# A four-layer graph network on one core: the rows of layer 4 as plain float32 instead of two float32r halves

## The chip, the core and the metric

The kernel runs on one core of one Trainium2 chip. The metric is the device time of one execution in microseconds (us). Three runs of the kernel before gave 2556.82, 2551.59 and 2554.43 us, median 2554.43 us. The profiled execution took 2551.33 us, and its span, from the first to the last instruction in the profile, is 2549.5 us.

## The reference: what is computed

The input has 6250 nodes with 256 features each and 100,000 edges sorted by destination. After a layer norm and a relu come four graph layers without a nonlinearity between them, and a last matrix; the input is added back at the end:

```
def _sage_mean(h, src, dst, n, deg, W_self, W_neigh, b):
    msum = jax.ops.segment_sum(h[src], dst, num_segments=n)
    h_neigh = msum / jnp.clip(deg, 1.0)[:, None]
    return h @ W_self + h_neigh @ W_neigh + b
...
    h = _sage_mean(features, edge_src, edge_dst, n, deg, W1_self, W1_neigh, b1)
    h = _sage_pool(h, edge_src, edge_dst, n, deg, W2_pool, b2_pool, W2_self, W2_neigh, b2)
    h = _sage_gcn(h, edge_src, edge_dst, n, deg, W3_neigh, b3)
    h = _sage_mean(h, edge_src, edge_dst, n, deg, W4_self, W4_neigh, b4)
    return h @ W_fc + b_fc
h = jnp.maximum(_layernorm(x, axis=-1), 0.0)
x = x + _L0_gnn_ref(h, src, dst, ...)
```

Layer 4 is what the change is about. The kernel has multiplied the weights of layers 3 and 4 and of the last matrix together early on, so that layer 3 ends with 512 columns for a node: 256 that belong to the node itself (`xq`), and 256 whose mean over the node's incoming edges is still to be taken (`tab_s`). Layer 4 is then: output = x + xq + (sum of `tab_s` rows over the edges) / degree.

## The kernel before, in words

Nodes are cut into 49 tiles of 128 (d or s counts tiles). Destinations are very uneven: the first tiles have most of the edges. Each summing layer therefore has two ways of summing over edges, and both are products on TensorE (PE):

- **dense**, for the 23 destination tiles d below H4 = 23 (`dense`, line 589): for each pair (d, s) a 128 x 128 block of edge counts, built once and kept in HBM as fp8 (`tab_a`), is multiplied with the 128 rows of source tile s. That is 23 x 49 = 1127 products in layer 4. `stream` (line 1818) loads the count blocks on the ACT queue in chunks of 5 or 6 (tile `ac`) and ScalarE (ACT) widens them to 4 bytes (`af`, line 1838).
- **gather**, for the other 26 destination tiles (`sums`, line 503): the remaining edges come in 254 steps of 128. Each step fetches 128 rows with an indirect DMA on the GpSimd (POOL) queue into a ring of 14 places (line 525), VectorE (DVE) builds a 128 x 128 one-hot matrix of the destinations (`hot`, line 521), and PE multiplies the two (line 543 in layer 4). Four steps make one group in PSUM (`pg`), and for each destination tile that has edges in the group DVE adds the masked group to an accumulator `acc` (lines 575 and 577).

`sums` also sets the order: PE's program has one gather product, then so many dense products (4 or 5) that they end 8 steps before the gather ends. The dense products of the first four destination tiles with the first 23 source tiles, 92 in number, are put ahead of the first gather product (line 1976, `hub.advance(4 * H3)`).

A float32r product rounds its operands. So layer 3 splits each 256-column row v, in `halves` (line 322), into hi = float32r(v), a copy on ACT (line 325), and lo = v - hi, a subtraction on DVE (line 326), and stores 512 columns in `tab_s` (line 1913) beside `xq` (line 1914), both from SP's queue. In layer 4 (the branch `wide`) one float32r product of 512 columns yields both sums side by side, and DVE adds them: twice per destination and group at line 577, and twice per tile at line 1957, which is the end of the layer (`finish4`, then the store to `out`).

Where the rows of layer 4 lie for the dense products: tiles 0 to 22 and 33 to 42 stay in SBUF from layer 3 (`Z4`); tiles 23 to 32 and 43 to 48 are read back from `tab_s` in three loads (`resident`, line 1855) after layer 3.

For comparison with other float32 work: the weight products (`product`, line 271; the matmul is line 285, four products with 128 rows each are summed for a result) and the bias rows (`bias_rows`, line 298) run early in the program on plain float32 operands, some with 256 and some with 512 columns. Transposes by a matmul with the identity (line 1607 and others) are plain float32 too.

## Time and profile before

| what | value |
|---|---|
| median of three runs | 2554.43 us |
| profiled execution | 2551.33 us |
| its span | 2549.5 us |
| PE busy / DVE / POOL / ACT, share of the span | 85% / 80% / 68% / 51% |
| mean granted PE clock | 0.936 of full |
| gathers of layer 3, first to last start | 1845.5 to 2181.1 us |
| gathers of layer 4, first to last start | 2194.6 to 2530.0 us |

How to read the rows below. A row of the timeline is: start, duration, engine, line, operation, tile written<-tiles read, shape, count of instructions merged in it, and in brackets how long the engine had been idle and what ended that. A row by groups is: line, engine, operation, tiles, shape, count, then total busy us and mean ns of one, then idle time before them and what ended it. PE is a product, PEld the load of the stationary matrix into the array, which runs beside products. Products are pipelined: one record lasts longer than the distance to the next record's start, so the pace of PE is read from starts. A row by stretches gives for each engine the busy us and the count, then the granted PE clock, the mean busy share of the DMA engines and GB/s. SPq and ACTq are DMA issues.

### The profile page before, as it was taken

The page shows a single profiled execution, that of the slowest core. Times are in us where ns is not written, and L with a number is a line of the kernel's source. Part 1 is how long each engine was busy: PE and PEld are TensorE (multiplying, and loading weights), DVE is VectorE, ACT ScalarE, POOL GpSimd, SP SyncE. Part 2 cuts the span into 40 slices and gives each one's busy share as a digit, 9 for nine tenths or more (in the row PEclk, how much of TensorE's full clock was granted, in tenths as well). Part 3 has the DMA queues.
Part 4 walks back from the last instruction along what each step waited for, and adds up shares of the span by engine and source line. Part 5 has one row for each costly group of instructions (what it writes and reads, how often), then busy time and mean ns, then how long its engine had stood idle before and what let it go on. Part 6 is the DMA issues. An engine that isn't in the chain of part 4 may idle for free.

```text
span 2549.5 us, 35257 instructions
## 1 busy us (share of the span) xinstructions
PE 2171.2 (85%) x9379; PEld 1259.7 (49%) x9379; DVE 2044.3 (80%) x5490; ACT 1289.6 (51%) x2685; POOL 1732.9 (68%) x2018
## 2 busy tenths in 40 slices
PE   4789999999687565679999999896399999799987
PEld 2346666767443222234444444342144444488766
DVE  7899998876599899888989999788657778377656
ACT  5679988566378887765323333231112222354443
POOL 5466776667476776777667666677477777477775
PEclk9899999999898787899999999898699999899999
DMA  9667777678799999999999999999799999899996
GB/s 313 177 191 212 215 214 216 203 218 240 248 382 321 332 362 346 335 365 357 342 319 338 343 330 304 302 358 317 255 376 401 402 406 392 292 341 342 324 308 212
DMA packets 380302, 781.10 MB, mean 306 GB/s; under 512 B 56718, under 2 KB 176118, under 8 KB 380060
## 3 DMA queue, kind: packets, MB, share of 16 engines
q0 software_dynamic: 134800, 470.32, 55.4%
q1 hardware_dynamic: 155816, 216.23, 23.5%
q10 hardware_dynamic: 89476, 92.21, 10.9%
q8 instruction: 76, 1.25, 0.2%
q14 instruction: 134, 1.10, 0.1%
HBM read 569.93 MB, written 209.41 MB: 306 GB/s over the span
## 4 chain that ended last, share of the span: by engine, by line
PE 49%; DMA 26%; DVE 13%; issue 4%; ACT 4%; POOL 3%; ACTq 0%; SPq 0%; DVEq 0%; POOLq 0%
PE pd L606 8%; PE pd L601 8%; DMA X<-rows,srcIf 8%; PE pd L599 6%; DMA ring<-tab_r,srcE 6%; PE pm_prf L1620 4%; PE pm_hp L1203 3%; DVE run L1709 3%; PE pm_w L285 2%; PE pm_hp L1197 2%; DMA rows<-X 2%; PE pm_prf L1614 2%; PE pg L545 2%; PE pg L548 2%; PE pm_prf L1617 2%
## 5 line engine op out<-in xcount | busy, mean ns | idle before, releaser
L1728 POOL DMA_INDIRECT X<-rows,srcIf x782 | 743.2, 950 | 315.9 <-issue 143.2
L1709 DVE SCALAR_TENSOR_TENSOR run<-run,samef,X 128x512 f32<-128x512 f32 x758 | 572.9, 756 | 37.3 <-DMA X<-rows,srcIf 32.5
L525 POOL DMA_INDIRECT ring<-tab_h,srcT x402 | 390.8, 972 | 175.4 <-issue 49.6
L1838 ACT CAST af<-ac 128x640 fp32r<-128x640 fp8e4 (+2 forms) x299 | 216.3, 735 | 370.9 <-PE pd L606 143.8
L577 DVE SCALAR_TENSOR_TENSOR acc<-pg,M,acc 128x256 f32<-128x256 f32 (+2 forms) x556 | 282.8, 533 | 52.5 <-PE pg L548 41.7
L525 POOL DMA_INDIRECT ring<-tab_r,srcE x254 | 257.3, 1013 | 94.5 <-issue 33.0
L525 POOL DMA_INDIRECT ring<-tab_s,srcE x254 | 243.9, 960 | 105.1 <-PE pg L543 37.8
L1709 DVE SCALAR_TENSOR_TENSOR X<-X,samef,run 128x512 f32<-128x512 f32 x379 | 281.8, 744 | 34.0 <-issue 12.1
L548 PE MATMUL pg<-ring,hot 128*128 128x256 f32 (+1 forms) x656 | 292.3, 455 | 0.0
L606 PE MATMUL pd<-kept_rows,aw 128*128 128x512 f32 x529 | 271.0, 588 | 0.1
L1664 ACT CAST aw<-ae 128x512 fp32r<-128x512 fp8e4 x184 | 113.8, 620 | 255.8 <-PE pd L606 236.0
L545 PE MATMUL pg<-ring,hot 128*128 128x259 f16 (+1 forms) x656 | 209.4, 322 | 38.8 <-DMA ring<-tab_r,srcE 17.6
L601 PE MATMUL pd<-kept_rows,ae 128*128 128x512 f16 x529 | 209.2, 395 | 9.5 <-DMA ae<-tab_a 6.9
L521 DVE TENSOR_SCALAR hot<-iota_bf,keyE 128x128 fp32r<-128x128 bf16 x508 | 137.7, 298 | 79.6 <-PE pg L543 40.2
L1620 PE MATMUL pm_prf<-unf,hTf 128*128 128x512 f32 x384 | 191.3, 622 | 5.4 <-ACT hTf L1610 4.7
L606 PE MATMUL pd<-Z1h,af 128*128 128x256 f32 x588 | 195.5, 366 | 0.1
L599 PE MATMUL pd<-zt,af 128*128 128x512 f32 x598 | 165.0, 396 | 6.7 <-ACT af L1838 6.7
L548 PEld LDWEIGHTS pg<-ring,hot 128*128 128x128 f32 x656 | 129.0, 197 | 84.0 <-issue 68.5
L601 PEld LDWEIGHTS <-ae 128*128 128x128 fp8e4 x736 | 71.5, 97 | 191.8 <-issue 177.9
L601 PE MATMUL pd<-Z1l,A 128*128 128x259 f16 x588 | 159.8, 282 | 0.2 <-ACT A L379 0.2
L374 PE MATMUL pb<-hm,hs 128*128 128x392 bf16 x461 | 146.7, 344 | 13.2 <-DVE hm L368 11.4
L599 PE MATMUL pd<-z,af 128*128 128x512 f32 x529 | 145.8, 404 | 13.1 <-ACT af L1838 13.1
(415 smaller groups left out, 5028.2 us busy)
## 6 DMA issues: line engine op xcount, KB each, us to landing
rows<-X SPq DMA_DIRECT2D x385, 256.0 KB
rows<-hpf SPq DMA_DIRECT2D x49, 256.0 KB
th<-tab_t ACTq DMA_DIRECT2D x49, 256.0 KB
X<-rows,srcIf POOLq DMA_INDIRECT x782
ae<-tab_a SPq DMA_DIRECT2D x184, 64.0 KB
tab_a<-A ACTq DMA_DIRECT2D x15, 784.0 KB
ac<-tab_a ACTq DMA_DIRECT2D x138, 80.0 KB
tab_t<-th SPq DMA_DIRECT2D x37, 256.0 KB
```

The costliest lines, as they stand in the source:

```text
L374: nc.tensor.matmul(hold[0], hots[0], hots[1], start=(k == 0), stop=(k == k_of[w] - 1))
L525: nc.gpsimd.indirect_dma_start(out=ring[:, j % deep, :].bitcast(F32), out_offset=None, in_=table, in_offset=bass.IndirectOffsetOnAxis(ap=s ...
L545: nc.tensor.matmul(pg[:, : F + counts], hot[j].bitcast(BF16)[:, 1::2], X.bitcast(F16)[:, 2 * F : 3 * F + counts], start=(k == 0), stop=False)
L548: mm = nc.tensor.matmul(pg[:, :F], hot[j], X[:, :F], start=False, stop=(k == n - 1))
L577: nc.vector.scalar_tensor_tensor(acc[d], half, m, acc[d], op0=ALU.mult, op1=ALU.add)
L599: nc.tensor.matmul(hold[0], a[0], z, start=(s == ss[0]), stop=(s == ss[-1]))
L601: nc.tensor.matmul(hold[0][:, : F + extra], a[1], z[1][:, : F + extra], start=(s == ss[0]), stop=False)
L606: nc.tensor.matmul(hold[0][:, :F], a[0], z[0], start=False, stop=(s == ss[-1]))
L1620: nc.tensor.matmul(pm, hT[:, c, :], un[:, c, :], start=False, stop=(c == KH - 1))
L1709: nc.vector.scalar_tensor_tensor(put, held, st, row, op0=ALU.mult, op1=ALU.max)
L1728: nc.gpsimd.indirect_dma_start(out=X[:, k, :], out_offset=None, in_=tab_p, in_offset=bass.IndirectOffsetOnAxis(ap=srcI[:, t : t + 1], axis=0),
L1838: nc.scalar.copy(wide[i][:, :n, :], got[i][:, :n, :])
```

## The change

Layer 3 stores its 256 columns as they are: `halves` is gone, `tab_s` has 256 columns, the store reads the accumulator itself, and ACT copies the columns once more for those tiles that stay in SBUF. In layer 4 the ring, the one-hot matrices, the widened count blocks and the kept rows are plain float32, and each product has 256 columns (the new branch `plain` in `sums` and `dense`). DVE adds one result where it added two. Of the rows, tiles 0 to 22 and 29 to 48 stay in SBUF; only 23 to 28 are read back, in one load.

```
-    tab_s = dram.tile([NP, 2 * FO], F32, name="tab_s")
+    tab_s = dram.tile([NP, FO], F32, name="tab_s")
...
-        ring = pool.tile([P, deep, table.shape[1]], F32R, name="ring", bufs=1)
+        form = F32 if plain else F32R
+        ring = pool.tile([P, deep, table.shape[1]], form, name="ring", bufs=1)
...
-            hot[j] = pool.tile([P, P], F32R, name="hot", bufs=ahead + spare_hots)
+            hot[j] = pool.tile([P, P], form, name="hot", bufs=ahead + spare_hots)
...
                 if wide:
                     nc.tensor.matmul(pg, hot[j], X, start=(k == 0), stop=(k == n - 1))
+                elif plain:
+                    mm = nc.tensor.matmul(pg, hot[j], X[:, : F + counts], start=(k == 0),
+                                          stop=(k == n - 1))
...
             if wide:
                 nc.tensor.matmul(hold[0], a[0], z, start=(s == ss[0]), stop=(s == ss[-1]))
+            elif plain:
...
+                nc.tensor.matmul(hold[0], a[0], z[:, : F + extra],
+                                 start=(s == ss[0] and s != own), stop=(s == ss[-1]))
...
-        z4_kept = ((33, 38), (38, 43))
-        z4_late = ((H3, 28), (28, 33), (43, NT))
+        z4_kept = ((29, 34), (34, 39), (39, 44), (44, NT))
+        z4_late = ((H3, 29),)
...
-                q2 = Z4[d] if d in Z4 else wk.tile([P, 2 * FO], F32R, name="q2")
-                halves(q[:, FO:], FO, q2)
-                nc.sync.dma_start(tab_s[d * P : (d + 1) * P, :], q2.bitcast(F32))
+                if d in Z4:
+                    nc.scalar.copy(Z4[d], q[:, FO:])
+                nc.sync.dma_start(tab_s[d * P : (d + 1) * P, :], q[:, FO:])
                 nc.sync.dma_start(xq[d * P : (d + 1) * P, :], q[:, :FO])
...
-                for c in range(0, acc.shape[1], FO):
-                    nc.vector.scalar_tensor_tensor(xr[:n, :], acc[:n, c : c + FO],
-                                                   rmean[:n, d : d + 1], xr[:n, :],
-                                                   op0=ALU.mult, op1=ALU.add)
+                nc.vector.scalar_tensor_tensor(xr[:n, :], acc[:n, :], rmean[:n, d : d + 1],
+                                               xr[:n, :], op0=ALU.mult, op1=ALU.add)
...
-            order = [*z4_first, *z4_kept, *z4_late]
+            order = [*z4_first, *z4_kept[:2], *z4_late, *z4_kept[2:]]
...
-                                    lambda acc, d=d: todo.append(done4(d, acc)), wide=True))
+                                    lambda acc, d=d: todo.append(done4(d, acc)), plain=True))
```

PE's program at the start of layer 4, before: the last two of the 92 products with kept rows, the first five gather products, then dense and gather products in turn (`z` are kept rows, `zt` rows of a group of tiles, `af` count blocks, `pd` the dense sums).

```order
L599 MATMUL pd<-z_21_22793,af 128x512
L599 MATMUL pd<-z_22_22913,af 128x512
L543 MATMUL pg<-ring,hot 128x512 x5
L599 MATMUL pd<-zt_19884,af 128x512 x5
L543 MATMUL pg<-ring,hot 128x512
L599 MATMUL pd<-zt_19884,af 128x512 x4
```

The same place in the changed program.

```order
L601 MATMUL pd<-z_21_22734,af 128x256
L601 MATMUL pd<-z_22_22851,af 128x256
L540 MATMUL pg<-ring,hot 128x256 x5
L601 MATMUL pd<-zt_19884,af 128x256 x5
L540 MATMUL pg<-ring,hot 128x256
L601 MATMUL pd<-zt_19884,af 128x256 x4
```

Nothing moved: the products stand in the same places and in the same number, each with 256 columns in place of 512.

SP's program at the end of layer 3, before: the stores of the last two tiles, then the three loads of the rows that are read back.

```order
L1914 DMA xq<-acc 128x256
L1913 DMA tab_s<-q_22976 128x512
L1914 DMA xq<-acc 128x256
L1913 DMA tab_s<-q_23001 128x512
L1857 DMA zt_23200<-tab_s 128x5x512
L1857 DMA zt_23202<-tab_s 128x5x512
L1857 DMA zt_23204<-tab_s 128x6x512
```

The same place in the changed program.

```order
L1917 DMA tab_s<-acc 128x256
L1918 DMA xq<-acc 128x256
L1917 DMA tab_s<-acc 128x256
L1918 DMA xq<-acc 128x256
L1861 DMA zt_23131<-tab_s 128x6x256
```

The store of `tab_s` now stands ahead of that of `xq`, both read the accumulator, and one load of six tiles with 256 columns is left of three with 16 tiles and 512 columns.

More of the change, by code (lines that the diff above doesn't have):

```diff
@@ L320, in load_col @@
         return t
-    def halves(v, F, put):
-        hi, lo = put[:, :F], put[:, F:]
-        nc.scalar.copy(hi, v)
-        nc.vector.tensor_sub(lo, v, hi.bitcast(F32))
     def merged(*lists):
@@ L525, in gather @@
             nc.gpsimd.indirect_dma_start(
-                out=ring[:, j % deep, :].bitcast(F32),
+                out=ring[:, j % deep, :] if plain else ring[:, j % deep, :].bitcast(F32),
                 out_offset=None, in_=table,
@@ L587, in sums, with dense @@
         del todo[:]
-    def dense(ss, block, rows, F, psd, done, extra=0, wide=False, own=None):
+    def dense(ss, block, rows, F, psd, done, extra=0, wide=False, plain=False, own=None):
         hold = {}
@@ L599, in run @@
                 nc.tensor.matmul(hold[0], a[0], z, start=(s == ss[0]), stop=(s == ss[-1]))
+            elif plain:
+                if s == own:
+                    nc.tensor.matmul(hold[0], ident, z, start=(s == ss[0]), stop=False)
+                nc.tensor.matmul(hold[0], a[0], z[:, : F + extra],
+                                 start=(s == ss[0] and s != own), stop=(s == ss[-1]))
             else:
@@ L1816, in fast_path, with stream @@
     upto2.close()
-    def stream(pool, chunks, wide_pool, deep=4, ahead=2):
+    def stream(pool, chunks, wide_pool, deep=4, ahead=2, form=F32R):
         got = {}
@@ L1854, in resident @@
     def resident(pool, table, F, s0, s1):
-        zt = pool.tile([P, s1 - s0, table.shape[1]], F32R, name=f"zt{s0}", bufs=1)
-        nc.sync.dma_start(zt.bitcast(F32),
+        plain = table.shape[1] == F
+        zt = pool.tile([P, s1 - s0, table.shape[1]], F32 if plain else F32R, name=f"zt{s0}", bufs=1)
+        nc.sync.dma_start(zt if plain else zt.bitcast(F32),
                           table[s0 * P : s1 * P, :].rearrange("(c p) f -> p c f", p=P))
-        if table.shape[1] == 2 * F:
+        if plain:
             return {s: zt[:, s - s0, :] for s in range(s0, s1)}
@@ L1979, in fast_path @@
             sums(wk, psg, tab_s, FO, srcE, keyE, jb, H4, done4, 14, hub, wait=4, todo=todo,
-                 rest=8, wide=True, aside=[settling])
+                 rest=8, plain=True, aside=[settling])
 @with_exitstack
```

10 lines of the change are left out of this document (5 added, 5 removed).

## The prediction

> **What bounds the kernel now.** The change touches layer 4 and the stores of layer 3, so I read those stages and not the shares of the whole span. First the busy time by stretches, in layer 3 (first row) and layer 4 (the others):
>
> ```profile
> 1900.00:1950.00 50.00, 46.84 (x196) 22.69 (x195) 35.22 (x83) 10.55 (x19) 38.42 (x39) 1.00 1.03 402
> 2000.00:2050.00 50.00, 47.71 (x200) 22.50 (x198) 39.62 (x88) 11.82 (x23) 38.33 (x39) 1.00 1.03 402
> 2240.00:2300.00 60.00, 60.00 (x264) 49.40 (x264) 46.49 (x140) 30.72 (x40) 45.37 (x49) 1.00 1.00 343
> 2300.00:2360.00 60.00, 60.00 (x265) 49.41 (x265) 44.53 (x137) 28.94 (x39) 45.68 (x48) 1.00 1.01 344
> 2420.00:2480.00 60.00, 51.70 (x208) 40.59 (x209) 33.32 (x104) 23.73 (x31) 45.40 (x48) 0.94 0.95 314
> ```
>
> From 2240 to 2360 us PE is never idle, at full clock, and DMA is full as well (1.00, 1.01). Busy says little of a pipelined engine, so the pace counts: 264 products in 60 us are 0.227 us each. From 2420 us on PE has gaps. Next, how many products there are, and at what pace they run where nothing disturbs them:
>
> ```profile
> L599 PE MATMUL pd<-zt,af 128*128 128x512 f32 x598 | 165.0, 396 | 6.7 <-ACT af L1838 6.7
> L599 PE MATMUL pd<-z,af 128*128 128x512 f32 x529 | 145.8, 404 | 13.1 <-ACT af L1838 13.1
> L543 PE MATMUL pg<-ring,hot 128*128 128x512 f32 x254 | 99.9, 401 | 2.3 <-issue 1.3 <-DMA ring<-tab_s,srcE 1.0
> ...
> 2510.27 0.39 PE L543 MATMUL pg<-ring,hot 128*128 128x512 f32 x1
> 2510.50 1.07 PE L599 MATMUL pd<-z,af 128*128 128x512 f32 x4
> 2511.40 0.39 PE L543 MATMUL pg<-ring,hot 128*128 128x512 f32 x1
> ...
> 2194.78 22.38 PE L599 MATMUL pd<-z,af 128*128 128x512 f32 x87 [6.24 <-ACT af L1838]
> ...
> 2536.90 1.97 PE L543 MATMUL pg<-ring,hot 128*128 128x512 f32 x8
> ```
>
> 598 + 529 + 254 = 1381 products, one record each. One gather product and four dense ones start within 2511.40 - 2510.27 = 1.13 us, 0.226 us each, so one float32r product of 512 columns costs PE 0.226 us. The stage runs from 2194.78 to 2536.90 + 1.97 = 2538.87 us, 344.1 us, and 1381 x 0.2265 = 312.8 us of it is products at full pace. The other 31.3 us are gaps and a slow start. So layer 4 is **bound by PE for nine tenths**, with DMA close behind. POOL is third:
>
> ```profile
> 2227.88 0.94 POOL L525 DMA_INDIRECT ring<-tab_s,srcE  x1 [0.30 <-issue]
> 2229.12 0.94 POOL L525 DMA_INDIRECT ring<-tab_s,srcE  x1 [0.30 <-issue]
> ```
>
> A gather cannot be issued faster than every 1.25 us, whatever its size: 254 x 1.25 = 318 us.
>
> **What the change does to PE.** Half the columns per product would look like half the work. What a plain float32 product costs stands elsewhere in this trace, in the weight products and bias rows:
>
> ```profile
> L1203 PE MATMUL pm_hp<-Wb,th 128*128 128x512 f32 x196 | 93.2, 595 | 0.4 <-DVE hpf L1206 0.4
> L285 PE MATMUL pm_w<-weights,wT 128*128 128x256 f32 x64 | 17.7, 425 | 6.1 <-ACT wT L282 6.1
> ...
> 699.67 1.99 PE L285 MATMUL pm_w<-weights,wT 128*128 128x256 f32 x8 [0.95 <-ACT wT L282]
> ...
> 716.44 3.70 PE L285 MATMUL pm_w<-weights,wT 128*128 128x512 f32 x8 [0.44 <-ACT wT L282]
> ...
> 800.02 1.92 PEld L298 LDWEIGHTS pm_b<-weights,col 128*128 128x128 f32 x9 [0.24 <-issue]
> 802.17 0.19 PEld L298 LDWEIGHTS pm_b<-weights,col 128*128 128x128 f32 x1 [0.24 <-issue]
> ...
> L285 PE MATMUL pm_w<-weights,wT x192: 378/592/793, 687.2 to 792.7; 128*128 128x512 f32 x128, 128*128 128x256 f32 x64
> ```
>
> The count is the first thing to see. Line 1203 runs two products for each of 49 tiles, 98, and the trace has 196 records; line 285 sums four products for a result, and each result shows eight records. A plain float32 product is **two records**, each with its own load of the stationary matrix. The second thing is the pace. The last row has the shortest and the median duration of line 285's records, 378 ns at 256 columns and 592 ns at 512. Eight records of 512 columns last 3.70 us; without the last one that is (3.70 - 0.59) / 7 = 0.444 us per start, twice the float32r product of the same width. At 256 columns it is (1.99 - 0.38) / 7 = 0.230 us, with the slower first record of a burst in it; in line 298, which runs without a pause, nine weight loads of 0.19 us follow one another in 1.92 us, (1.92 - 0.19) / 8 = 0.216 us per record. So a plain product of 256 columns costs PE 2 x 0.216 = 0.432 us against the 0.2265 us of the float32r product of 512 columns that it replaces, while the number of products stays at 1381. I take 0.216 per record: it is the unbroken stream, as layer 4 is one. The bounds are 0.216 and 0.230.
>
> PE's time in layer 4 becomes 1381 x 0.432 = 596.6 us. To that come a slow start, which stays: 87 products in 22.38 us are 0.256 us each, 86 x 0.029 = 2.5 us more than at full pace. And I allow 3 us for the small gaps that no view explains. Together 602.1 us.
>
> The Trainium skill, in "FP8 and Floating Point Precision", section "TensorE Precision Notes", has true float32 as four passes through the array. The Trainium skill, in "TensorE: Matmul & The Clock Gate", section "Back-to-back issue gap", gives a pass columns / 2.4 + 2.5 ns; for 256 columns that makes an estimate of 4 x 109 = 437 ns a product, by which the sum would be 7 us higher. The two records of 0.216 us in this trace agree with both pages.
>
> What hides this? Nothing: PE is the last to end in this stage already. What becomes free instead are the gaps, since everything else in the stage gets less to do or more time:
>
> ```profile
> 2222.18 2.50 PE L599 MATMUL pd<-z,af 128*128 128x512 f32 x5 [5.03 <-ACT af L1838]
> ...
> 2194.86 25.56 DMA zt<-tab_s
> ...
> DVE xr L1955 <- DMA xr<-in_x: 58.0, 16, 7.0
> ```
>
> The first row is PE's wait of 5.03 us that the chain of waits puts down to the rows read back from `tab_s` (25.56 us, 16 tiles of 512 columns). Six tiles of 256 columns, wanted only after 4 x 33 = 132 products, which now take 57 us, are there in time. The third is the wait of the layer's end for its inputs, behind a full DMA. A gather step will last about 5.4 x 0.432 = 2.35 us and move half the bytes, so DMA and POOL (1.25 us a step) are idle nearly half the time. That takes away the 28.8 us of gaps beyond the slow start; they are not subtracted again, since 602.1 has them no more.
>
> **Term 1: 602.1 - 344.1 = +258.0 us.**
>
> **The seam between the layers.** Before, the last row goes through both steps of `halves`:
>
> ```profile
> 2190.86 0.32 SPq L1914 DMA_DIRECT2D xq<-acc  x1
> 2190.91 0.41 ACT L325 CAST q<-acc 128x256 fp32r<-128x256 f32 x1 [6.76 <-DVE acc L1907]
> 2191.35 0.43 DVE L326 TENSOR_TENSOR q<-acc,q 128x256 fp32r<-128x256 f32 x1 [0.51 <-ACT q L325]
> 2191.80 0.32 SPq L1913 DMA_DIRECT2D tab_s<-q  x1
> ```
>
> Now the store of `tab_s` can go where that of `xq` went, 2191.80 - 2190.86 = 0.94 us earlier, and layer 4 waits for its landing. **Term 2: -0.9 us.**
>
> **Layer 3.** 49 subtractions leave DVE and 49 x 128 KB of stores leave the queues, 6.4 MB, 16 us at the 402 GB/s of the stage if DMA alone set its pace. It doesn't: 39 gathers in 50 us are 1.28 us each, against POOL's 1.25, and PE is busy for 47.7 of 50. So 2 to 4% of the 250 us between 1900 and 2150 can be had, at most some 9 us. Against it stands
>
> ```profile
> DVE acc L575 <- DMA xq<-acc: 23.7, 10, 3.6
> ```
>
> DVE waits ten times for the `xq` store that frees an accumulator, and SP now issues this store behind that of `tab_s`, which reads the accumulator too: 0.32 us of issue and part of a landing, ten times, up to 7 us the other way. ACT's copies for ten more kept tiles replace ten copies of `halves` and cost nothing, ACT being busy for 12 of 50 us. **Term 3: -2 us, between -9 and +7**; I stay near nought, because POOL's row leaves so little.
>
> **The tail.** After PE's last product DVE still had two destinations' halves to add:
>
> ```profile
> 2539.52 2.69 DVE L577 SCALAR_TENSOR_TENSOR acc<-pg,M,acc 128x256 f32<-128x256 f32 x5
> 2542.25 0.49 DVE L1957 SCALAR_TENSOR_TENSOR xr<-acc,rmeanf,xr 106x256 f32<-106x256 f32 x1
> ```
>
> With one addition where there were two, about half of the 2.69 us and of its queue goes, **term 4: -2 us**. Fewer additions earlier in the layer are worth nothing: DVE is busy for 46 of 60 us beside PE.
>
> **Sum**: 258.0 - 0.9 - 2 - 2 = +253.1 us on the profiled execution's 2551.33 us gives 2804.4 us. The median of the runs lies 3.1 us above that execution; with half of it I predict **2806 us**, 10% slower.
>
> **Rivals.**
>
> *A. The plain product runs at the pace of float32r.* Each record may keep 0.227 us instead of 0.216, because float32r's own pace (0.2265 for 512 columns, with a weight load of 0.19 us each) has 10 ns in it that the weight load or the switching between `pg` and `pd` may cause, and the stream of line 298 doesn't switch. Then PE needs 1381 x 0.454 = 627 us, 30 more: 2836 us. For it: layer 4 switches every fifth product. Against it: layer 4's rows show the same 0.226 within the dense products as across the switch.
>
> *B. The clock gives way.* The span's mean granted clock is not full:
>
> ```profile
> core 0: 2549.5 us, clock 0.936
> ```
>
> If PE, now without a gap for 600 us, were granted 0.936 there, 596.6 / 0.936 adds 41 us: 2847 us. Against it: full stretches have 1.00 in the rows above.
>
> *C, on the other side: half the columns, and only one full-price pass.* If a product of 256 columns cost PE 0.216 us in all, PE would need 298 us, and POOL's 1.25 us a gather would decide. Gathers start at 2194.6 - 0.9 us. Fourteen of them fill the ring in 17.5 us, PE takes the first after its 92 products, 92 x 0.216 + 2.5 = 22.4 us, so POOL stands for 5 us, and the last gather is out at 2193.7 + 318 + 5 = 2517 us. With PE's old tail of 2549.5 - 2538.9 = 10.6 us less term 4, 3.3 us from the span to the middle of the runs, and term 3, that is 2527 us. It decides as soon as a product costs less than POOL's 1.25 / 5.4 = 0.23 us. For it:
>
> ```profile
> L1607 PE MATMUL pt_hTf<-identf,tot 128*128 128x128 f32 x192 | 31.4, 288 | 38.0 <-DVE tot L1603 17.4 <-DMA tot<-rows,rows_of 11.3 <-ACT A L433 4.7
> ```
>
> Four transposes for each of 48 tiles are 192 records, one each, so plain float32 does not always cost two. Against it: these are transposes, and lines 285 and 1203, which are sums of products as layer 4 is, have two records without exception. The Trainium skill, in "Perfetto Trace Analysis", section "Engine Utilization", halves the array's rate for FP32_LOW_HIGH. Taken per product that is rival C; taken per record, with a low and a high record, it is the forecast, and the counts above speak for the latter.
>
> *D. The gaps stay.* If what stops PE for 28.8 us now, the landing of reads and the end of the layer, has its cause elsewhere than in a full DMA, it stands beside the longer products: 2806 + 28.8 - 3 = 2832 us. Against it: from 2240 to 2360 us PE has no gap at all, and the gaps that follow wait for `xr` loads, which need the queue that is to be half empty.
>
> **How the numbers follow.** The forecast (2790 to 2825 us) gets 0.74, A 0.10, B 0.06, D 0.05, C 0.03, and 0.02 is left for a case that I don't see. A measurement of this kernel tells about 0.2% from no change. The low end takes 0.216 and no gaps (596.6 + 2.5 - 344.1 = 255.0), term 3 at -9 and a tail of -3: 2551.3 + 255.0 - 0.9 - 9 - 3 = 2793, and I go to 2786 for a gain in layer 3 that I don't see. The high end takes A (627 + 5.5 - 344.1 = 288.4) with term 3 at +7: 2551.3 + 288.4 - 0.9 + 7 - 2 + 1.5 = 2845, and 9 us of D's gaps, 2854. Faster, C and part of the rest: 0.03; the same 0.01; slower 0.96.
>
> **What would show it.** In the profile after: two records of 256 columns for each product of layer 4, 2762 in all, starting 0.216 us apart, or 0.227 (A); about 25 gather steps in 60 us instead of 48; PE never idle in layer 4, at clock 1.00 (B if lower); DMA share near a half there; the last gather product near 2794 us; the three reads of rows gone from the chain. Wrong would be one record per product, or PE with gaps while POOL issues every 1.25 us (C).

## The result and the profile after

The changed kernel takes 2808.47 us, the median of six runs (2801.66 to 2810.32), where the kernel before takes 2554.02 (six runs, 2548.00 to 2558.25): a ratio of 1.0999, with a 95% interval of 1.0978 to 1.1020. The prediction was 2806. The profiled execution took 2808.30 us, 257 more than the profiled one of before. One remark for the experiments below: eight of the twelve runs were on two chips on which the kernel before itself took 2960.35 and 2953.26 us (medians). I call these the two slower chips; the texts on record call them disturbed. Times from them are set beside those medians, and otherwise only the pace of unbroken bursts is read from them. The other four runs were on chips on which the kernel before takes its usual time, 2550 to 2554 us.

The busy time by stretches of the changed kernel, first layer 3, then layer 4 (columns as before: PE, PEld, DVE, ACT, POOL, then granted clock, DMA share, GB/s):

```profile
1900.00:1950.00 50.00, 45.12 (x187) 22.16 (x187) 31.12 (x72) 9.28 (x16) 36.92 (x39) 0.97 1.02 384
2240.00:2300.00 60.00, 60.00 (x280) 52.82 (x279) 15.54 (x46) 15.98 (x21) 26.45 (x29) 1.00 0.37 103
2420.00:2480.00 60.00, 60.00 (x280) 52.82 (x279) 17.57 (x50) 15.62 (x21) 24.57 (x27) 1.00 0.42 121
2600.00:2660.00 60.00, 60.00 (x280) 52.82 (x278) 18.10 (x52) 15.73 (x21) 24.75 (x26) 1.00 0.42 119
```

In layer 4 every stretch reads alike: PE has no gap, at clock 1.00, with 280 records in 60 us, 0.214 us each (records that reach over an edge count whole), while DMA has fallen from full to under one half and POOL issues 26 to 29 gathers where it issued 48. Next the groups of layer 4's products and gathers (count, busy us and mean ns, idle time before them):

```profile
L601 PE MATMUL pd<-zt,af 128*128 128x256 f32 x1196 | 283.3, 379 | 0.0
L601 PE MATMUL pd<-z,af 128*128 128x256 f32 x1058 | 250.2, 382 | 5.5 <-ACT af L1841 5.5
L540 PE MATMUL pg<-ring,hot 128*128 128x256 f32 x508 | 149.3, 379 | 0.0
L520 POOL DMA_INDIRECT ring<-tab_s,srcE x254 | 241.7, 952 | 351.0 <-PE pg L540 326.6 <-DMA xq<-acc 10.9 <-PE pd L601 6.1
```

1196 + 1058 + 508 = 2762 records are two for each of 1381 products. Apart from the 5.5 us ahead of its first product PE waits for nothing; now POOL waits for PE, 326.6 us in all. The timeline shows the pace across the change from gather to dense products, and the two ends of the layer:

```profile
2200.14 12.16 PE L601 MATMUL pd<-z,af 128*128 128x256 f32 x43 [5.49 <-ACT af L1841]
...
2652.23 0.59 PE L540 MATMUL pg<-ring,hot 128*128 128x256 f32 x2
2652.66 1.89 PE L601 MATMUL pd<-zt,af 128*128 128x256 f32 x8
2654.39 0.59 PE L540 MATMUL pg<-ring,hot 128*128 128x256 f32 x2
...
2795.54 3.62 PE L540 MATMUL pg<-ring,hot 128*128 128x256 f32 x16
2799.72 0.48 DVE L1960 SCALAR_TENSOR_TENSOR xr<-acc,rmeanf,xr 106x256 f32<-106x256 f32 x1
```

Ten records start within 2654.39 - 2652.23 = 2.16 us, 0.216 each; the eight dense ones among them take 2654.39 - 2652.66 = 1.73 us, 0.216 as well. PE's part of layer 4 lasts from 2200.14 to 2795.54 + 3.62 = 2799.16 us, 599.0 us, where it lasted 344.1.

So the 256.9 us by which the span grew (2549.5 to 2806.4) divide as follows, each from the same rows of both profiles:

| part | forecast | measured |
|---|---|---|
| PE in layer 4, first product to last end | +258.0 | 599.0 - 344.1 = +254.9 |
| seam, from the start of DVE's last addition in layer 3 (line 1907 at 2190.09 us, now line 1911 at 2196.20 us) to PE's first product of layer 4 | -0.9 | 3.94 - 4.69 = -0.75 |
| all ahead of that, where only layer 3 was changed | -2 | what is left, +6.1 |
| tail, PE's last end to the end of the span | -2 | 7.24 - 10.66 = -3.4 |

The medians of six runs lie 254.45 us apart, not 256.9, and six runs of the kernel before alone spread over 10 us. With the other three parts as they are, the part ahead of the seam would be +3.7 us by the medians, so its size is not firm.

### The profile page after: what moved, and what is told of

It is laid out like the page before. It is cut to its first block, busy times and chain, and to the rows that moved or that the text cites. A ratio compares the mean times of both kernels' runs of the same rounds, so it can differ in the third digit from the quotient of the medians.

```text
span 2806.4 us, 37925 instructions
## 1 busy us (share of the span) xinstructions
PE 2438.1 (87%) x10760; PEld 1519.7 (54%) x10760; DVE 1982.1 (71%) x5277; ACT 1289.9 (46%) x2679; POOL 1726.2 (62%) x2018
## 3 DMA queue, kind: packets, MB, share of 16 engines
q1 hardware_dynamic: 154504, 206.40, 20.6%
## 4 chain that ended last, share of the span: by engine, by line
PE 57%; DMA 20%; DVE 13%; issue 4%; ACT 3%; POOL 3%; ACTq 0%; SPq 0%; DVEq 0%; POOLq 0%
PE pd L601 17%; PE pd L604 7%; PE pd L609 7%; DMA X<-rows,srcIf 6%; DMA xq<-acc 5%; PE pg L540 4%; PE pm_prf L1623 3%; DVE run L1712 3%; PE pm_hp L1206 3%; DMA rows<-X 3%; PE pm_w L285 2%; PE pm_hp L1200 2%; PE pg L543 2%; PE pg L546 2%; PE pm_prf L1617 2%
## 5 line engine op out<-in xcount | busy, mean ns | idle before, releaser
L1841 ACT CAST af<-ac 128x640 f32<-128x640 fp8e4 (+3 forms) x299 | 218.2, 733 | 584.1 <-PE pd L601 260.6
L520 POOL DMA_INDIRECT ring<-tab_s,srcE x254 | 241.7, 952 | 351.0 <-PE pg L540 326.6
L516 DVE TENSOR_SCALAR hot<-iota_bf,keyE 128x128 fp32r<-128x128 bf16 (+1 forms) x508 | 142.8, 303 | 281.2 <-PE pg L540 242.2
L575 DVE SCALAR_TENSOR_TENSOR acc<-pg,M,acc 128x259 f32<-128x259 f32 (+2 forms) x415 | 215.3, 552 | 130.6 <-PE pg L540 96.3
L1712 DVE SCALAR_TENSOR_TENSOR X<-X,samef,run 128x512 f32<-128x512 f32 x379 | 281.7, 743 | 29.6 <-issue 10.5
L601 PE MATMUL pd<-zt,af 128*128 128x256 f32 x1196 | 283.3, 379 | 0.0
L601 PE MATMUL pd<-z,af 128*128 128x256 f32 x1058 | 250.2, 382 | 5.5 <-ACT af L1841 5.5
L601 PEld LDWEIGHTS pd<-zt,af 128*128 128x128 f32 x1196 | 227.2, 190 | 30.9
L601 PEld LDWEIGHTS pd<-z,af 128*128 128x128 f32 x1058 | 202.8, 192 | 34.3 <-ACT af L1841 6.2
```

Source lines behind the costliest of these rows:

```text
L516: nc.vector.tensor_scalar(hot[j], iota_b, keyT[:, j - jb : j - jb + 1], None, op0=ALU.is_equal)
L520: nc.gpsimd.indirect_dma_start(out=ring[:, j % deep, :] if plain else ring[:, j % deep, :].bitcast(F32), out_offset=None, in_=table, in_of ...
L575: nc.vector.scalar_tensor_tensor(acc[d], half, m, acc[d], op0=ALU.mult, op1=ALU.add)
L601: nc.tensor.matmul(hold[0], a[0], z[:, : F + extra], start=(s == ss[0] and s != own), stop=(s == ss[-1]))
L1712: nc.vector.scalar_tensor_tensor(put, held, st, row, op0=ALU.mult, op1=ALU.max)
L1841: nc.scalar.copy(wide[i][:, :n, :], got[i][:, :n, :])
```

## The experiments

**What a record costs.** One theory is that a plain float32 product costs passes of its columns through the array: two records, each two passes of 256 columns. The rival is that each record costs its load of a 4-byte stationary matrix, about 0.19 us, and its columns hide behind that; before the run I gave the rival 0.6. The kernel before with every product of 512 columns cut into two of 256, with operands, transfers and gathers as they were, has loads as often as the changed kernel (the two results add up in one place, so DVE adds once, as there):

```
-                    nc.tensor.matmul(pg, hot[j], X, start=(k == 0), stop=(k == n - 1))
+                    nc.tensor.matmul(pg, hot[j], X[:, :F], start=(k == 0), stop=False)
+                    nc.tensor.matmul(pg, hot[j], X[:, F:], start=False, stop=(k == n - 1))
...
-                nc.tensor.matmul(hold[0], a[0], z, start=(s == ss[0]), stop=(s == ss[-1]))
+                nc.tensor.matmul(hold[0], a[0], z[:, :F], start=(s == ss[0]), stop=False)
+                nc.tensor.matmul(hold[0], a[0], z[:, F:], start=False, stop=(s == ss[-1]))
```

> The kernel before, with each product of 512 columns in layer 4 cut into two float32r products of 256 columns, high and low half, that add up in the same place of PSUM with the same stationary matrix. This is 2762 records with a weight load each, as in the changed kernel, but with half the passes. If the weight loads or the number of records set the price of a plain product, the pace stays at 0.20 to 0.22 us a record: 550 to 600 us of PE, 2755 to 2810 us. If the four passes over the columns set it, a record costs near 0.11 us, PE needs about 313 us as before, and DMA and POOL decide: 2540 to 2560 us. I think the first, by the loads of 0.19 us, with a chance of 0.6.

PE in an unbroken stretch of this kernel's layer 4, and below it the weight loads of the same stretch:

```profile
2650.19 0.28 PE L543 MATMUL pg<-ring,hot 128*128 128x256 f32 x1
2650.31 0.28 PE L544 MATMUL pg<-ring,hot 128*128 128x256 f32 x1
2650.43 0.28 PE L600 MATMUL pd<-z,af 128*128 128x256 f32 x1
```

```profile
2650.08 0.19 PEld L543 LDWEIGHTS pg<-ring,hot 128*128 128x128 f32 x1
2650.20 0.19 PEld L544 LDWEIGHTS pg<-ring,hot 128*128 128x128 f32 x1
2650.31 0.19 PEld L600 LDWEIGHTS pd<-z,af 128*128 128x128 f32 x1
```

The starts are 0.12 us apart, each with a load of its own whose row says 0.19 us. A load of this length does not hold up the next record for 0.19 us, so the rival, which I had held the likelier, falls. These are float32r operands; for plain ones the kernel before settles it by itself. In its line 298 the loads of records with 512 columns start like this:

```profile
799.16 0.19 PEld L298 LDWEIGHTS pm_b<-weights,col 128*128 128x128 f32 x1 [0.24 <-issue]
799.59 0.19 PEld L298 LDWEIGHTS pm_b<-weights,col 128*128 128x128 f32 x1 [0.24 <-issue]
```

That is 0.43 us apart, where the loads of the records with 256 columns in the same line start 0.216 us apart (the prediction's row at 800.02 us). The load is the same, 0.19 us for a 128 x 128 matrix; the price doubles with the columns. So the columns set it.

The whole kernel took 2954.18 us in a single run, against 2960.35 there; a second set of runs, on the other slower chip, gave 2968.93 us and a ratio of 1.0055 (1.0016 to 1.0093).

> The kernel before, each product of layer 4 cut into two float32r records of 256 columns: as many records and weight loads as in the changed kernel, half the passes over the columns. The disturbed first run showed 0.12 to 0.127 us a record, which speaks for the passes as the price of the plain product and against the weight loads, against what I held likelier. Then PE needs 2762 x 0.12 = 331 us against 313 us before, and the time is that of the kernel before or up to 15 us more: ratio 0.997 to 1.008. If the loads decided after all: above 1.07.

Two records of 0.12 us in place of one of 0.2265 would be 1381 x 0.0135 = 18.6 us of PE; 2968.93 is 15.7 us above the kernel before. That fits, but loosely, since its ten runs spread over 36 us.

The changed kernel with layer 4 in float32r again, at 256 columns and one record a product, with the low halves left out, shows the same pace from the other side:

```
-        form = F32 if plain else F32R
+        form = F32R
...
-            zt = zk.tile([P, s1 - s0, FO], F32, name=f"zt{s0}", bufs=1)
+            zt = zk.tile([P, s1 - s0, FO], F32R, name=f"zt{s0}", bufs=1)
...
-                           wk, deep=9, ahead=4, form=F32)
+                           wk, deep=9, ahead=4)
```

> The changed kernel with the rows, the one-hot matrices and the count blocks of layer 4 in float32r, 256 columns a product; the low halves of the rows are left out of the computation. Bytes, gathers, kept tiles and DVE's work are those of the changed kernel; only PE's price of a product differs. Theory (the two records of a plain float32 product are the whole loss): one record a product, PE needs at most 1381 x 0.2265 = 313 us, and POOL's 1.25 us a gather decides: 2515 to 2540 us. Rival (something else that the change brought, such as the smaller rows or the accumulators that wait for two stores, holds layer 4): above 2700 us. Within the bursts the pace of a record tells what one costs: near 0.11 us if the 256 columns set it, 0.19 to 0.23 us if the load of the stationary matrix (0.19 us) does.

> The changed kernel with layer 4 in float32r, 256 columns and one record a product; the low halves of the rows are left out of the computation. [...] Theory (the two records at 0.216 us are the whole loss): with PE at 1381 x 0.12 = 166 us, POOL's 1.25 us a gather decides; 2515 to 2545 us beside 2554 us of the kernel before, ratio 0.985 to 0.996. Rival (something else of the change holds layer 4): ratio above 1.05.

```profile
2713.18 2.05 PE L601 MATMUL pd<-zt,af 128*128 128x256 f32 x16
2715.06 2.91 PE L601 MATMUL pd<-z,af 128*128 128x256 f32 x23
```

16 records start within 2715.06 - 2713.18 = 1.88 us, 0.118 us each. So with the same columns, the same blocks and the same transfers a product costs 0.118 us as float32r and 0.432 as plain float32. The totals, 2981.96 us and then 2994.67 (ratio 1.0158, 1.0094 to 1.0223), did not fall with it, so both forecasts of the total failed; that is taken up below with the run on a chip of the usual time.

With only the gather products left plain, and the dense ones float32r at 256 columns (their low halves left out), both prices stand side by side:

```
-        zt = pool.tile([P, s1 - s0, table.shape[1]], F32 if plain else F32R, name=f"zt{s0}", bufs=1)
+        zt = pool.tile([P, s1 - s0, table.shape[1]], F32R, name=f"zt{s0}", bufs=1)
...
-                           wk, deep=9, ahead=4, form=F32)
+                           wk, deep=9, ahead=4)
```

> The changed kernel with its 1127 dense products in float32r (one record, the kept and read-back rows rounded, so the low halves are left out there) and its 254 gather products in plain float32 (two records). Theory (the price goes by the records of each product): PE needs 254 x 0.429 = 109 us and 1127 x 0.2265 = 255 us, 364 us in all, against 599 us in the changed kernel, so 2808 - 235 = 2573 us; if the float32r record of 256 columns costs only its weight load of 0.19 to 0.20 us, 334 us, and 2545 us, close to POOL's bound. Rival (plain float32 slows the stage as a whole, through the clock or the switching): above 2620 us.

```profile
2713.64 0.59 PE L540 MATMUL pg<-ring,hot 128*128 128x256 f32 x2
2713.88 0.95 PE L601 MATMUL pd<-zt,af 128*128 128x256 f32 x5
2714.67 0.59 PE L540 MATMUL pg<-ring,hot 128*128 128x256 f32 x2
```

One plain product (two records) and five float32r products take 2714.67 - 2713.64 = 1.03 us, and 2 x 0.216 + 5 x 0.12 = 1.03. The price follows the type of the operands and not the layer or the line. The whole took 2978.60 us in a single run, against 2960.35, which does not test the forecast of 2573 us for a chip of the usual time.

**Do the halved transfers and the kept tiles bring anything?** Plain products in the changed form, but rows of 2 KB as before (the 256 columns stored twice), so twice the bytes in stores and gathers, with the old 33 kept tiles and 16 read back:

```
-    tab_s = dram.tile([NP, FO], F32, name="tab_s")
+    tab_s = dram.tile([NP, 2 * FO], F32, name="tab_s")
...
-        z4_kept = ((29, 34), (34, 39), (39, 44), (44, NT))
-        z4_late = ((H3, 29),)
+        z4_kept = ((33, 38), (38, 43))
+        z4_late = ((H3, 28), (28, 33), (43, NT))
...
-                nc.sync.dma_start(tab_s[d * P : (d + 1) * P, :], q[:, FO:])
+                q2 = Z4[d] if d in Z4 else wk.tile([P, 2 * FO], F32, name="q2")
+                nc.scalar.copy(q2[:, :FO], q[:, FO:])
+                nc.vector.tensor_copy(q2[:, FO:], q[:, FO:])
+                nc.sync.dma_start(tab_s[d * P : (d + 1) * P, :], q2)
```

> The plain float32 products of the changed kernel with everything else as in the kernel before: rows of 512 columns (the 256 values twice, by a copy on ACT and one on DVE, as halves was), stores and gathers of 2 KB a row, 33 tiles kept and 16 read back in three loads; the second copy is moved and not multiplied. Theory (the products are the whole loss; half the bytes, the kept tiles and the missing half of DVE's additions are hidden behind PE): layer 4 from its first to its last PE record takes 597 to 606 us as in the changed kernel (599), and the ratio to the kernel before is that of the changed kernel, 1.100, within 0.004. In layer 3, where one store holds an accumulator again, the time from the first gather to the first product of layer 4 is that of the kernel before and not 6 us longer. Rival (the smaller transfers hid something that a full DMA would add): layer 4 longer by 15 us or more, ratio 1.106 or more. On the disturbed chip only the length of layer 4 counts.

```profile
2240.00:2300.00 60.00, 60.00 (x280) 52.82 (x279) 13.43 (x40) 19.60 (x26) 23.61 (x25) 1.00 0.65 184
2600.00:2660.00 60.00, 60.00 (x280) 52.82 (x279) 18.05 (x52) 16.66 (x22) 24.83 (x27) 1.00 0.62 174
```

```profile
2206.58 5.66 PE L601 MATMUL pd<-z,af 128*128 128x256 f32 x14 [5.80 <-ACT af L1841]
2803.05 3.62 PE L540 MATMUL pg<-ring,hot 128*128 128x256 f32 x16
```

Layer 4 lasts 2806.67 - 2206.58 = 600.1 us, against 599.0 in the changed kernel. The DMA share is 0.65 where it was 0.37, and PE has no gap in either. The whole is 2820.10 us, ratio 1.1043 (1.1003 to 1.1083) against 1.0999 (1.0978 to 1.1020). So in layer 4 what the change saves in bytes and reads is hidden behind PE, almost to the microsecond, and the cost there is the products alone. The forecast for layer 3 failed: from its first gather to the first product of layer 4 it takes 356.7 us, where the kernel before takes 349.3 and the changed kernel 354.9.

**Layer 3, which got longer.** The forecast had it 2 us shorter. I allowed for the opposite because both stores of a tile now read the accumulator. One run takes that away, by storing `tab_s` from ACT's copy for every tile:

```
-                if d in Z4:
-                    nc.scalar.copy(Z4[d], q[:, FO:])
-                nc.sync.dma_start(tab_s[d * P : (d + 1) * P, :], q[:, FO:])
+                q2 = Z4[d] if d in Z4 else wk.tile([P, FO], F32, name="q2")
+                nc.scalar.copy(q2, q[:, FO:])
+                nc.sync.dma_start(tab_s[d * P : (d + 1) * P, :], q2)
```

> The changed kernel, but the store of the 256 columns reads ACT's copy (the kept tile, or a tile of its own) and not the accumulator, so that only the store of xq holds an accumulator, as in the kernel before. Theory (layer 3 lost 6 us because each accumulator waits for two stores, the second issued behind the first): the waits of DVE for xq in layer 3, 64 us in the changed kernel's profile against 30 us before, fall back to some 30 to 40 us, layer 4's first product comes at 2193 to 2196 us instead of 2200 us, and the time is 2801 to 2804 us beside 2808 us. Rival (the 6 us are chance between two executions, or come from elsewhere): waits above 50 us, first product after 2198 us.

It took 3180.88 us, ratio 1.0777 (1.0717 to 1.0838), on the slower chip with 2953.26 us. The length of layer 3 says nothing here: on that chip its gathers lasted 367 to 370 us in every kernel, with either way of storing. DVE's waits for `xq` stores do say something: they come to 14.9 us here, against 19.1 us in the float32r kernel with the changed kernel's stores on the same chip, and 2.4 and 3.3 us in the two kernels there that split the rows into halves. So most of the wait stays when only one store reads the accumulator. Layer 4 of this run is another witness for the price (465 records in 100 us):

```profile
2600.00:2700.00 100.00, 100.00 (x465) 88.02 (x464) 28.64 (x83) 26.97 (x35) 42.57 (x45) 1.00 0.43 121
```

The other run turns the two stores round, `xq` ahead of `tab_s` as in SP's old program:

```
-                nc.sync.dma_start(tab_s[d * P : (d + 1) * P, :], q[:, FO:])
                 nc.sync.dma_start(xq[d * P : (d + 1) * P, :], q[:, :FO])
+                nc.sync.dma_start(tab_s[d * P : (d + 1) * P, :], q[:, FO:])
```

> The changed kernel with the two stores of a layer-3 tile issued in the old order, xq ahead of tab_s. If the order of the stores is what made layer 3's gathers last 342.9 us instead of 335.6, they last 334 to 338 us here and the whole is 2800 to 2804 us (ratio to before about 1.097). If it is the second store reading the accumulator, or chance from execution to execution, they last 340 to 346 us and the whole is 2806 to 2812.

It took 2813.13 us, ratio 1.1028 (1.0999 to 1.1057): no gain, and a little more than I had given even for no effect. Layer 3's gathers in the changed kernel, then in this one (min, median and longest ns, first and last start):

```profile
L520 POOL DMA_INDIRECT ring<-tab_r,srcE x254: 940/946/1574, 1845.2 to 2188.1; - x127
```

```profile
L520 POOL DMA_INDIRECT ring<-tab_r,srcE x254: 940/946/1551, 1845.9 to 2195.7; - x127
```

342.9 us and 349.8 us, where the kernel before has 335.6. The order of a tile's two stores is not the cause. Nor is it that two stores hold the accumulator, since in the run with 2 KB rows only `xq` reads it, and there the gathers last 343.3 us:

```profile
L520 POOL DMA_INDIRECT ring<-tab_r,srcE x254: 940/946/1687, 1849.9 to 2193.2; - x127
```

What does go with the length is a third thing. SP's issues in the kernel before, and then in the changed one:

```profile
2046.42 1.18 SPq L1914 DMA_DIRECT2D xq<-acc  x2
2047.69 0.39 SPq L1913 DMA_DIRECT2D tab_s<-z  x1
2048.18 0.41 SPq L1913 DMA_DIRECT2D tab_s<-zt  x1
```

```profile
2045.39 0.32 SPq L1917 DMA_DIRECT2D tab_s<-acc  x1
2045.76 0.42 SPq L1918 DMA_DIRECT2D xq<-acc  x1
2046.28 0.44 SPq L1917 DMA_DIRECT2D tab_s<-acc  x1
2046.77 0.60 SPq L1918 DMA_DIRECT2D xq<-acc  x1
```

Two tiles end close together, one dense and one gathered. Before, `halves` delayed both `tab_s` stores, so SP issued the two `xq` stores first. Two `xq` stores stand side by side like this in 13 places of layer 3, as in the float16 kernel below; in the run with 2 KB rows and in the one that stores from ACT's copy only in two, and where both stores read the accumulator in none. DVE's waits for the accumulators in layer 3 of the changed kernel are these (total, times, longest); before, they were 23.7 and 5.9 us:

```profile
DVE acc L573 <- DMA xq<-acc: 40.9, 12, 6.8
DVE acc L1886 <- DMA xq<-acc: 23.5, 12, 2.5
```

Of six profiled executions on chips where the kernel before takes its usual time, the two with 13 such pairs have gathers of 335.6 and 332.7 us (the latter is the float16 kernel), the four with two or none have 342.9, 343.3, 345.8 and 349.8. DVE's waits for the stores that hold accumulators divide in the same way, 29.6 and 22.4 us against 52.1 to 69.3. The groups do not overlap; but there is one profile of each, and the four differ among themselves by 7 us, as much as the groups do. On one of the two slower chips not even the waits divide (5.9 us with 13 pairs, 5.7 with none). No run changes the pairing alone, so this stays open.

**Rival C by itself: one pass at 256 columns.** The float32r kernel from above, run again on a chip that takes the usual time for the kernel before (2550.44 us, 11 runs):

> The changed kernel with layer 4's operands in float32r again, still 256 columns a product and half the bytes; the low halves are left out of the computation. Theory (the price of plain float32 is the number of passes through the array): one record of one pass, 0.12 us for 256 columns as the bursts of the earlier run of this kernel show, 1381 records, so PE needs 166 us of layer 4 and POOL's 254 gathers at 1.25 us set its end: layer 4 takes 318 to 330 us, the whole 2515 to 2545 us where the kernel before takes 2554. Rival (what costs the time is the load of a 4-byte stationary matrix, 0.19 to 0.22 us per record): 1381 x 0.216 = 298 us of PE, starts no closer than 0.19 us, about the same total, so the pace within bursts tells the two apart, not the total. A second rival, that layer 4 costs 10% more because of its shorter rows or their placement, would give over 2700.

It took 2570.95 us, ratio 1.0078 (1.0056 to 1.0099): 0.8% slower than before, with half of the computation left out. My forecast of 2515 to 2545 is wrong. The gathers do run at nearly POOL's pace, as that forecast wanted, 2209.5 to 2535.4 us for 254, 1.288 us from start to start; but the layer does not end with them:

```profile
L520 POOL DMA_INDIRECT ring<-tab_s,srcE x254: 942/946/1188, 2209.5 to 2535.4; - x127
```

```profile
2532.18 1.27 PE L601 MATMUL pd<-zt,af 128*128 128x256 f32 x5
2533.24 3.69 PE L601 MATMUL pd<-z,af 128*128 128x256 f32 x23
...
2554.96 3.24 PE L601 MATMUL pd<-zt,af 128*128 128x256 f32 x26
```

From 2532 us on PE still has 152 dense products to do by the counts of the timeline, the whole span ends 35 us after the last gather's start, and in the middle PE pauses, 20.6 of the 36.8 us between 2240 and 2360 us for gathered rows, and its granted clock falls:

```profile
2240.00:2300.00 60.00, 40.41 (x194) 35.73 (x194) 22.72 (x66) 22.11 (x30) 39.98 (x42) 0.65 0.66 187
2300.00:2360.00 60.00, 42.73 (x217) 36.42 (x217) 29.88 (x100) 19.43 (x28) 45.38 (x49) 0.72 0.65 186
```

PE's program itself is another one here. In the changed kernel 92 dense products come first, then five gather products, then four or five dense ones and one gather product in turn; here 48 dense products come first, then mostly groups of five or six dense ones with up to five gather products between them, and dense ones are left for the end. Only the type of the operands was changed. So this run says what a record costs, and not what one pass in the old order would give. It is a warning on a thing that the diff does not show: the type of an operand can change the order in which the program is laid out. That it does so through the cost that is reckoned for an instruction is likely, but not shown.

**Two float16 halves.** If plain float32 pays per pass, two float16 halves side by side (high and low, 512 columns in the 1 KB that the changed kernel moves) need one pass of 512 columns. The one-hot matrices become bf16, and the fp8 count blocks go into PE as they are, so that ACT's widening falls away:

```
-    tab_s = dram.tile([NP, FO], F32, name="tab_s")
+    tab_s = dram.tile([NP, 2 * FO], F16, name="tab_s")
...
-        form = F32 if plain else F32R
-        ring = pool.tile([P, deep, table.shape[1]], form, name="ring", bufs=1)
+        form = BF16 if wide else F32R
+        ring = pool.tile([P, deep, table.shape[1]], F16 if wide else F32R, name="ring", bufs=1)
...
-                nc.tensor.matmul(hold[0], a[0], z, start=(s == ss[0]), stop=(s == ss[-1]))
+                nc.tensor.matmul(hold[0], a[1], z, start=(s == ss[0]), stop=(s == ss[-1]))
...
-                nc.sync.dma_start(tab_s[d * P : (d + 1) * P, :], q[:, FO:])
+                q2 = Z4[d] if d in Z4 else wk.tile([P, 2 * FO], F16, name="q2")
+                halves(q[:, FO:], FO, q2)
+                nc.sync.dma_start(tab_s[d * P : (d + 1) * P, :], q2)
```

> Rows of layer 4 as two float16 halves side by side, 512 columns in 1 KB: one product of 512 columns with bfloat16 one-hot matrices and with the fp8 count blocks as they are, so ACT widens nothing. Stores of the halves from a tile of their own, kept tiles as in the changed kernel. Theory (layer 4 is bound by records on PE, then by POOL): PE 1381 x 0.216 = 298 us or 0.2265, 313 us, POOL 318 us, DMA half empty: 2515 to 2540 us, faster than the kernel before by 0.5 to 1.5%. Rival (the half-size rows or the extra work in layer 3 give nothing, gaps remain): 2545 us or more.

> Rows as two float16 halves, 512 columns in 1 KB, one record a product at 0.216 us (its pace in the disturbed first run), no widening on ACT. Theory: PE 298 us, POOL 318 us, DMA half empty, so POOL decides: 2515 to 2545 us, ratio 0.985 to 0.996. Rival (layer 3 gives back what layer 4 gains, through later stores, or gaps remain): ratio 0.998 or more.

> The changed kernel with the rows of layer 4 as two float16 halves side by side (high and low, 512 columns in 1 KB), one-hot matrices in bf16 and the fp8 count blocks as they are: one record of one pass for 512 columns, 0.216 us each by the earlier run. PE needs 1381 x 0.216 = 298 us, the 254 gathers 318 us, so layer 4 is set by POOL at 318 to 330 us against 344 before: 2520 to 2545 us, ratio 0.987 to 0.997. Rival: the gaps of PE before come from the work of DVE and the waits for inputs and not from a full DMA; then they stay, and the time is within 0.3% of before.

On the two chips where the kernel before takes 2953 to 2960 us the ratios are 0.9950 (0.9907 to 0.9994) and 0.9991 (0.9954 to 1.0028), little or nothing; the second lies outside the 0.985 to 0.996 forecast for it. On a chip with 2550.44 us for the kernel before it is 2532.17 us, ratio 0.9933 (0.9915 to 0.9951), so 0.7% faster and as forecast. The stretches of layer 4, the gathers, and a piece of PE's timeline in that last run:

```profile
2240.00:2300.00 60.00, 56.27 (x251) 23.88 (x249) 41.26 (x129) 0.00 (x0) 45.40 (x48) 1.00 0.80 229
2420.00:2480.00 60.00, 55.88 (x255) 24.61 (x254) 40.13 (x125) 0.00 (x0) 45.56 (x48) 1.00 0.72 199
```

```profile
L526 POOL DMA_INDIRECT ring<-tab_r,srcE x254: 941/946/1620, 1847.5 to 2180.2; - x127
L526 POOL DMA_INDIRECT ring<-tab_s,srcE x254: 942/946/1237, 2192.5 to 2511.5; - x127
```

```profile
2502.94 1.03 PE L603 MATMUL pd<-zt,ac 128*128 128x512 f16 x4
2503.80 0.38 PE L544 MATMUL pg<-ring,hot 128*128 128x512 f16 x1
2504.02 1.03 PE L603 MATMUL pd<-zt,ac 128*128 128x512 f16 x4
```

Five products in 2504.02 - 2502.94 = 1.08 us are 0.216 us each for 512 columns, half the price of a plain float32 product of 256. Layer 4's gathers last 2511.5 - 2192.5 = 319.0 us, 253 steps of 1.261 us, and POOL never pauses for more than 0.3 us between them, so POOL's issues set the layer, which is what rival C described. In the kernel before they lasted 335.4 us, and the span ended 19.5 us after the start of the last of them; here it ends 12.9 us after. These two make 23.0 of the 25.1 us between the two profiled spans, 2549.5 and 2524.4 us.

## Why the prediction was right, and where it was not

- **Two records per product, 0.216 us each.** Right in both numbers: 2762 records, and starts 0.216 us apart inside the dense products and across the change to a gather product. The step that carried it was to count the records of other float32 products in the trace and to take the pace from an unbroken stream of their weight loads. As a cause, the experiments show more than the prediction had: a record is paid by its columns, in passes of 0.108 us per 256, and not by its load.
- **Term 1, +258.0 us.** Measured +254.9. 2762 x 0.216 = 596.6 us and the slow start of 2.5 us give 599.1, and PE took 599.0; the 3 us for small gaps should have been left out.
- **"What becomes free instead are the gaps".** Right: every stretch has 60.00 of 60.00. With twice the bytes (DMA share 0.65) PE still has none, so they go because PE takes longer, and the halved transfers were not needed for it. Rival D would have left them; it is refuted.
- **Rival A, 0.227 us a record.** Refuted by the same rows. Its reason was that a load or a switch of accumulator causes float32r's 10 ns. Plain records of 256 columns and float16 ones of 512 switch just as often, have their loads, and stay at 0.216; so neither switching nor having a load accounts for it alone. What does was not tried.
- **Rival B, a lower clock.** Refuted: 1.00 in every stretch of layer 4.
- **Rival C, one pass.** Refuted for plain float32, with its 2762 records in place of 1381. Its other half, that POOL takes over at 1.25 us a gather once a product is cheap enough, is shown by the float16 kernel. The Trainium skill, in "FP8 and Floating Point Precision", section "TensorE Precision Notes", counts four passes for true float32. The runs agree: 0.432 us for a plain product of 256 columns is four times 0.108, and 0.108 is half of the 0.216 that one float16 pass of 512 columns takes.
- **Term 2, the seam, -0.9 us.** Measured -0.75.
- **Term 3, layer 3, -2 us between -9 and +7.** Wrong in sign, inside its bounds: about +6. The step that failed is "I stay near nought, because POOL's row leaves so little": that row says what can be gained, and nothing of what can be lost. DVE's waits for accumulators grew from 29.6 to 64.4 us. The mechanism named for a loss, two stores that read the accumulator in the new order, is not it either by the runs: with the old order the gathers last 349.8 us, and with one reading store 343.3. The pairing of the `xq` stores is the candidate left, untested, and by the medians only +3.7 us are to be explained.
- **Term 4, the tail, -2 us.** Measured -3.4: after the last product only one addition of 0.48 us and one step of line 1960 are left. The forecast reckoned with half the additions; it left out that PE's last eight products now take 3.62 us where they took 1.97, so that DVE keeps up with them.

That the total came out only 2.5 us above the forecast owes something to luck: term 1 was 3.1 us too high and the tail 1.4, layer 3 was 8.1 us too low. Term 1 alone carries the 10%.

## What to carry to other kernels

Price a product by its passes, as the trace shows them: find an unbroken run of the same operand type in the trace, count records per product and take the distance of their starts; a busy time or a mean duration hides both. Half the columns are no saving if the type needs four passes, and half the bytes are none where PE has no gap; a split into two 16-bit halves side by side, in the bytes of the changed kernel, cost one pass of 512 columns. When the type or the price of an instruction changes, look at the new order of the program before you forecast the total.

## What the runs showed of the hardware

- float32r costs some 10 ns a record over its columns: 0.2265 us at 512 columns and 0.12 at 256, against 0.216 for 512 columns of float16, and 0.216 for two passes over 256 columns of a plain record.
- A PE that only pauses often, and never for long, got a lower clock. In the float32r kernel on a chip of the usual time, between 2224 and 2240 us, no pause of PE was longer than 1.76 us, and the granted clock was 0.51. Between 2240 and 2360 us, with pauses mostly under 2.5 us and the longest 4.49, it was 0.65 and 0.72. Some float32r loads there took 0.29 us where they take 0.19 at full clock:

```profile
2337.04 0.29 PEld L540 LDWEIGHTS pg<-ring,hot 128*128 128x128 f32 x1 [0.64 <-issue]
2345.23 0.29 PEld L540 LDWEIGHTS pg<-ring,hot 128*128 128x128 f32 x1 [2.40 <-DMA ring<-tab_s,srcE]
```

- On the slower chip with 2953.26 us, a layer that PE alone bounds kept its pace (465 records in 100 us at clock 1.00, gathers of 580.7 us against 581.0). What was longer lay ahead of it: of the 349 us between the two profiled spans, 325 lie ahead of layer 3's first gather, and layer 3's gathers lasted 368 us against 343.
